# A transformer layer's tail: the last batch's state-space inputs made by channel tiles, its attention moved behind its first scan step, the experts' buffers moved

## The chip, the cores and the metric

The kernel runs on one core of a Trainium2 chip. A core has a matmul engine (TensorE, PE in the profile), a vector engine (VectorE, DVE), an activation engine (ScalarE, ACT), a general engine (GpSimd, POOL), a queue processor for transfers (SyncE, SP), and DMA engines that all of them share. Each engine runs its instructions in the order in which the program lists them, and semaphores hold an instruction until what it needs is done. The metric is the device time of one execution, in microseconds (us).

## The reference, cut to what matters

The input is `x`, 4 batches of 256 tokens with 256 channels. Three parts are added to it in turn, each on a layer norm of the sum so far:

1. A cross-attention of 8 heads: each batch's tokens look at 4096 context rows and at themselves.
2. A routed part. A small router scores the tokens of a batch. The best 64 go through an attention of 16 heads among themselves (`_attn_core`), the other 192 through a state-space layer (`_ssm_core`).
3. A mixture of 8 experts, of which each token takes 2.

```python
def _ssm_core(u, ...):
    xi, z = jnp.split(u @ in_w, 2, axis=-1)              # 512 channels each
    xc = conv_b + sum((xp[:, j:j + L] * conv_w[:, j] for j in range(DC)))
    xc = jax.nn.silu(xc)
    proj = xc @ xproj_w                                  # dtp (16), Bm (16), Cm (16)
    delta = jax.nn.softplus(dtp @ dt_w + dt_b)
    dA = jnp.exp(delta[..., None] * A)
    dBu = (delta * xc)[..., None] * Bm[:, :, None, :]
    # h = dA_t * h + dBu_t over the 192 tokens; y_t = sum over 16 states of h * C_t
    y = jnp.moveaxis(ys, 0, 1) + xc * Dp
    return (y * jax.nn.silu(z)) @ out_w
```

The experts are `silu(x @ gate) * (x @ up)` and then `@ down`, weighted and summed over the two experts of a token. All of it is fp32.

## The kernel before

**Tiling.** Channels or tokens lie on the 128 partitions. The 512 channels of the state-space layer are four channel tiles (`NDT`), m = 0 to 3, of 128 channels by 192 tokens, kept side by side in one tile of 128 x 768 (`xc`, `zs`, `delta`, `y`).

**The planner.** The cross-attention is a hand-written loop over 128 pieces of work. Beside it runs a list of Python generators (`active`), each of which issues some instructions and then yields how much later it is due, and how much room on VectorE its next step asks for. `slot(budget)` gives due generators their turn. The "time" here is only a counter (`now`), which the writer advances by an estimate at each piece. So the yields decide where instructions stand in each engine's order, and nothing else.

**The batches.** `routed(b)` is the generator of one batch's second part: `router`, `ssm_front`, the scan, `ssm_back`. `attention` is a generator beside it. Batches 0 to 2 lie under the cross-attention of the later batches. The last batch's part can only start when the cross-attention ends, and is called `late` in the code. `sortable` and `dispatch` sort the tokens of batches 0 to 2 by expert into 19 blocks of 128 rows (`NB`).

**The tail.** After the cross-attention come two loops. `ordered` runs the 19 sorted blocks. `experts` runs the last batch's 256 tokens through all 8 experts in turn ("dense"); it needs `x4T`, which `prepare` makes at the end of the last batch's second part. The last batch's generators run in the slots of `ordered`. For a block j the steps are:

- `load(j)`: three weight transfers of 512 KB on SP's queue (gateT, upT, downT, L1559), the expert's number read from a register that the block's entry is loaded into; three buffers each.
- `gather(j)`: GpSimd fetches the block's 128 rows (xg, L1597), 4 buffers.
- `turn_block(j)`: two transposes (psxb, L1609) and a copy on ScalarE (xTb, L1612).
- `half(j, 0)` and `half(j, 1)`: gate and up, p0b and p1b (L1618).
- `gated`: a tanh on ScalarE (sg, L1568), two VectorE instructions (L1569, L1573, the result is hb). In this text one such pair on VectorE is a gating.
- `down(j)`: pdb (L1632), a copy yb (L1639), and a store to ysd on SP's queue (L1640). In program order, `down(j - 1)` stands behind the gating of block j, and `load(j + 2)` behind that.

**The last batch before the scan.** `finish_batch` adds the last psx product of the cross-attention (L1392, added at L1400). `router` then normalises the tokens (L183 to L211), transposes them (psxn, L250; xnT, L255), scores them (psh, pssc; gelu at L273), ranks them on VectorE (L278 to L300), counts positions (psn, L306) and permutes (psg, L331), which gives `ua` (L336). `ssm_front` makes psin (L533) for each m, evicts it into xc and zs (L537, L541), adds the convolution (L508), and then works on all four channel tiles at once: tanh (L544) and silu (L546), projection (pspr, L553), the store bcd of B and C (L560), the gate of z (L563, L568), psdt (L579), ReLU and Abs on ScalarE (L586), exp and ln (L591, L592), delta (L594), the y products (L598) and delta times xc (L601). `attention` waits only for `ua`, so it runs in between: psqk (L378), kbd (L395), psva, psas (L419), the softmax (amx, pa, asm), psat, psao, psoT, psad, dsort.

**The late scan.** `ssm_scan_late` does 16 steps, four groups of four states (k) by four channel tiles (m). ScalarE makes the decay (L706), VectorE the rest:

```python
nc.vector.tensor_tensor(db, spread[k, 0], bc(xc[:, m, :], 1, SG), ALU.mult)   # L738
nc.vector.tensor_tensor_scan(out=db, data0=das[i % 2], data1=db, ...)         # L739
nc.vector.tensor_tensor(db, db, spread[k, 1], ALU.mult)                       # L745
nc.vector.tensor_tensor(db[:, :SG//2], db[:, :SG//2], db[:, SG//2:], ALU.add) # L746
```

TensorE sums the states into yps (L714). The rows of B and C come spread over the partitions by DMA from bcd (`spread`, tiles bbl and cbl, L696). `ssm_back` adds yps to y (L761), multiplies by the gate (L764), multiplies by out_w (pssd, L769), permutes back (psback, L779) and adds to x (L784); `prepare` normalises and transposes (psx at L1705).

**Memory.** Pools are laid out one behind the other, and those of the tail (`fp`, `fw`, `fk`, `late`) lie over those of the cross-attention: context rows (`ctx`, 16 KB a partition), then a pool `wk` with keys, values and transposed probabilities.

Of the kernel before, what the change touches and what calls it, by code (L numbers as in the profile page):

```python
# [8 lines left out]
F32 = mybir.dt.float32  # L9
AF = mybir.ActivationFunctionType  # L10
ALU = mybir.AluOpType
# [3 lines left out]
P = 128  # L15
B, T, D = 4, 256, 256
S = 4096
NT = B * T // P
KD = D // P
# [5 lines left out]
NBOT = T - KTOP  # L25
DIN, DS, DC, DTR = 512, 16, 4, 16
NDT = DIN // P
# [19 lines left out]
def perceiver_layer(ctx: ExitStack, tc: tile.TileContext, a: dict, out: bass.AP):  # L47
    nc = tc.nc
# [4 lines left out]
    bg = ctx.enter_context(tc.tile_pool(name="bg", bufs=1))  # L53
# [35 lines left out]
    cs = {}  # L89
# [132 lines left out]
    def bank(name):  # L222
        return ps_m.tile([P, 512], F32, tag="m", name=name)
# [8 lines left out]
    def router(b, st):  # L232
# [1 line left out]
        xb = x_sb[:, 2 * b : 2 * b + 2, :]  # L234
        mv = moments(xb)
        rs = scales(mv, twice=True)
        yield 2.5, 0.4
        nm = offsets(mv, rs)
        one = small.tile([P, 2], F32, name="one")
        nc.vector.tensor_scalar_add(one, rs[:, 0], 1.0)  # L240
        xn2 = bg.tile([P, 2, D], F32, tag="r1", name="xn2")
        scaled(xn2, xb, rs[:, 1], nm[:, 1])
        scaled(xb, xb, one, nm[:, 0])
        yield 2.5, 0

        xnT = bg.tile([P, KD, T], F32, tag="r2", name="xnT")
        ps = bank("psxn")
# [14 lines left out]
            out=lower, in_=lower, compare_op=ALU.is_gt, fill=0.0, base=0,  # L262
            pattern=[[P, 2], [-1, T]], channel_multiplier=1,
        )
        yield 2.0, 0
        hs = bg.tile([P, 2, T], F32, tag="r3", name="hT_srow")
        hT, srow = hs[:, 0, :], hs[:, 1, :]
        ps = bank("psh")
# [2 lines left out]
                ps[:, :T], cs["r_w1"][:, c, :], xnT[:, c, :], start=(c == 0), stop=(c == KD - 1)  # L271
            )
        nc.scalar.activation(hT, ps[:, :T], AF.Gelu_apprx_tanh, bias=cs["r_b1"])  # L273
        yield 3.0, 2.7

        ps = bank("pssc")
        nc.tensor.matmul(ps[:, :T], cs["r_w2"][:, 0, :].to_broadcast([P, P]), hT, start=True, stop=True)
# [10 lines left out]
        for h in range(2):  # L288
            eq = bg.tile([P, T], F32, tag="r4", name="eq")
            for other, op0, op1 in (  # L290
                (lower[:, h, :], ALU.is_equal, ALU.mult), (eq, ALU.is_gt, ALU.add),
            ):
                nc.vector.scalar_tensor_tensor(
                    out=eq, in0=srow, scalar=scol[:, h : h + 1], in1=other, op0=op0, op1=op1
                )
            nc.vector.tensor_reduce(out=rank[:, h : h + 1], in_=eq, axis=AX.X, op=ALU.add)
            if h == 0:
                yield 0.5, 1.6
        top = small.tile([P, 2], F32, name="top")
        nc.vector.tensor_scalar(  # L300
            out=top, in0=rank, scalar1=float(KTOP), scalar2=None, op0=ALU.is_lt
        )
        yield 1.0, 1.4

        ps = bank("psn")
        nc.tensor.matmul(ps[:, 0:1], cs["tri"], top[:, 0:1], start=True, stop=True)  # L306
# [13 lines left out]
        nc.vector.tensor_tensor(  # L320
            perm, bc(cs["posid"], 1, 2), bc(pos, 2, T), ALU.is_equal
        )
        yield 3.0, 0

        while late and "ready" not in order:
            yield 1.0, 0
# [32 lines left out]
    def attention(b, st):  # L359
# [6 lines left out]
        awq = weight("awq")  # L366
        yield early(b), 0
        awk = weight("awk")
        while "ua" not in st:
            yield 2.0, 0  # L370
        ua, dsort = st["ua"], st["dsort"]
        yield 3.0, 0
# [109 lines left out]
    def ssm_front(b, st):  # L482
# [34 lines left out]
        while "ua" not in st:  # L517
            yield 2.0, 0
        ua = st["ua"]
        yield 2.0, 0  # L520
        pss = {}
        for m in range(NDT + 1):
# [38 lines left out]
            out=bcd.rearrange("o s t -> (o s) t"), in_=projT[DTR:, :]  # L561
        )
        nc.scalar.activation(delta, zs, AF.Tanh)  # L563
        if late:
            st["late"] = ssm_scan_late(b, st)
            next(st["late"])
        yield 2.0, 1.0
        nc.vector.scalar_tensor_tensor(  # L568
            out=zs, in0=delta, scalar=1.0, in1=zs, op0=ALU.add, op1=ALU.mult
# [27 lines left out]
        for m in range(NDT):  # L597
            nc.scalar.activation(  # L598
                y[:, m, :], xc[:, m, :], AF.Copy, scale=cs["Dp"][:, m : m + 1]
            )  # L600
        (nc.vector if late else nc.gpsimd).tensor_tensor(xc, xc, delta, ALU.mult)  # L601

    def ssm_scan(b, st):

# [73 lines left out]
    def ssm_scan_late(b, st):  # L678

        SG = 4
        K = DS // SG
        pool = late["pool"]
        xc, delta = st["xc"], st["delta"]
# [14 lines left out]


        def decay(i):
            k, m = divmod(i, NDT)
            if k < K:
                for s in range(SG):
                    nc.scalar.activation(  # L706
                        das[i % 2][:, s, 1:], delta[:, m, 1:], AF.Exp,
                        scale=cs["amat"][:, m, SG * k + s : SG * k + s + 1],
                    )

        def sums(i):
# [12 lines left out]
        zero = pool.tile([P, SG, NBOT], F32, tag="dbl", name="zero", bufs=3)[:, :2]  # L724
        nc.gpsimd.memset(zero, 0.0)
        for i in range(2):
            nc.tensor.matmul(
                yps[:, i, : 2 * NBOT], ident, zero.rearrange("p s t -> p (s t)"),
                start=True, stop=False,
            )  # L730
        yield 0.0, 0
        decay(0)
        yield 1.0, 3.8
        for i in range(K * NDT):
            k, m = divmod(i, NDT)
            decay(i + 1)
            db = dbl[i] = pool.tile([P, SG, NBOT], F32, tag="dbl", name="db", bufs=3)
            nc.vector.tensor_tensor(db, spread[k, 0], bc(xc[:, m, :], 1, SG), ALU.mult)  # L738
            nc.vector.tensor_tensor_scan(  # L739
                out=db.rearrange("p s t -> p (s t)"),  # L740
                data0=das[i % 2].rearrange("p s t -> p (s t)"),
                data1=db.rearrange("p s t -> p (s t)"),
                initial=0.0, op0=ALU.mult, op1=ALU.add,
            )
            nc.vector.tensor_tensor(db, db, spread[k, 1], ALU.mult)  # L745
            nc.vector.tensor_tensor(db[:, : SG // 2], db[:, : SG // 2], db[:, SG // 2 :], ALU.add)  # L746
            if i:
                sums(i - 1)
            if m == NDT - 1:
                load(k + 2)  # L750
            yield 3.9, 3.8
        sums(K * NDT - 1)
        yield 1.5, 0
# [304 lines left out]
    def start(g):  # L1058
        active.append([g, now[0], 0.0])
# [479 lines left out]


    with ExitStack() as s4, tc.manual_schedule():
        fp = s4.enter_context(tc.tile_pool(name="ffn", bufs=1))
        fw = s4.enter_context(tc.tile_pool(name="ffw", bufs=3))
        fk = s4.enter_context(tc.tile_pool(name="ffk", bufs=3))
        ps_g = s4.enter_context(tc.tile_pool(name="ps_g", bufs=3, space=PSUM))
        late["psum"] = s4.enter_context(tc.tile_pool(name="ps_y", bufs=1, space=PSUM))
# [30 lines left out]
        def ordered():  # L1577
# [15 lines left out]

            def gather(j):
                if j < NB:
                    xgs[j] = fp.tile([P, D], F32, tag="xg", name="xg", bufs=4)
                    nc.gpsimd.indirect_dma_start(  # L1597
                        out=xgs[j], out_offset=None, in_=x4d,
                        in_offset=bass.IndirectOffsetOnAxis(
                            ap=order["tokens"][:, j : j + 1], axis=0  # L1600
                        ),
                    )

            def turn_block(j):
# [22 lines left out]
            def down(j):  # L1627
# [12 lines left out]
                nc.sync.dma_start(out=ys[j * P : (j + 1) * P, :], in_=y)  # L1640
                yield 0.86

            for j in range(4):
                gather(j)
            for j in range(3):
                load(j)
            for _ in range(6):
                yield 1.0
            turn_block(0)
            for j in range(NB):  # L1650
                pg = yield from half(j, 0)
                pu = yield from half(j, 1)
                turn_block(j + 1)
                hs[j] = fk.tile([P, NHC, P], F32, name="hb")
                gated(pg, pu, hs[j].rearrange("p m i -> p (m i)"), 512)
                gather(j + 4)
                yield 0.5
                yield from down(j - 1)
                if j:
                    load(j + 2)  # L1660
            yield from down(NB - 1)

            start(collect(NSORT, ys, order["slots"], order["weights"]))
# [168 lines left out]
```

## Time and profile before

| | us |
|---|---|
| median of 3 runs | 1555.44 (1549.75 to 1558.04) |
| the profiled execution | 1555.58, span 1553.9, mean clock 0.977 |
| last values matmul of the cross-attention ends | 1274.15 |
| last batch: last psx product added (L1400) | 1275.53 |
| last batch: ua done | 1308.6 |
| first multiply of the late scan (L738) | 1356.7 |
| last add of the late scan (L746) ends | 1443.1 |
| first matmul of the dense experts (L1749) | 1462.5 |

All stage times are microseconds from the start of the span. In the views of the profile, a row of the stages gives the stretch, its length, and then for each engine its busy time with the number of instructions in brackets. PEclk is the TensorE clock that was granted, as a part of full speed. A row of the chain of waits gives start, length, and the engine, tile and line that the end of the program hung on at that time. PEld is the loading of a matmul's stationary operand. "SPq" is SP's queue of transfers.

### The profile page before, as it was taken

To read this page: it belongs to the slowest core of one execution; us is meant where nothing else is said; L and a number is where in the kernel's file an instruction comes from. 1 tells how busy PE (TensorE), PEld (TensorE's weight loads), DVE (VectorE), ACT (ScalarE), POOL (GpSimd) and SP (SyncE) were. 2 spreads that over 40 slices of the span, in tenths; PEclk is the share of its full clock that TensorE was granted. 3 is DMA by queue.
4 is the path that set the end of the run, shared out by engine and by line. 5 is a ranking of instruction groups with operands and counts; after the bars stand their busy time and mean duration, and the time that the engine had idled before them with its cause. 6 is when DMAs were issued, how large, how long until landed. Compare 5 with 4: busy or idle time off the path is not lost.

```text
span 1553.9 us, 37283 instructions
## 1 busy us (share of the span) xinstructions
PE 1461.9 (94%) x15686; PEld 1039.5 (67%) x15686; DVE 1057.1 (68%) x1812; ACT 758.9 (49%) x1486; POOL 412.0 (27%) x464
## 2 busy tenths in 40 slices
PE   7999999999999999999999999999998868988799
PEld 3757667576667475766665767757665558778587
DVE  1666666666699976565999866658988633499453
ACT  3444454454666644555667454546664413534211
POOL 1000000000089940000799500005996011110100
PEclk9999999999999999999999999999999968999899
DMA  7445543524344525243454343334543115777471
GB/s 240 149 131 160 161 139 107 180 72 143 120 147 140 182 83 192 79 145 100 141 176 158 113 144 126 99 112 162 159 127 114 42 55 183 253 250 259 125 233 48
DMA packets 157767, 223.41 MB, mean 144 GB/s; under 512 B 14976, under 2 KB 76160, under 8 KB 157600
## 3 DMA queue, kind: packets, MB, share of 16 engines
q1 hardware_dynamic: 152368, 211.45, 42.7%
q10 hardware_dynamic: 3744, 5.51, 1.1%
q0 software_dynamic: 1488, 4.07, 0.9%
q8 instruction: 124, 2.03, 0.5%
q14 instruction: 43, 0.35, 0.1%
HBM read 216.56 MB, written 4.42 MB: 142 GB/s over the span
## 4 chain that ended last, share of the span: by engine, by line
PE 63%; POOL 14%; DVE 13%; issue 4%; ACT 3%; DMA 2%; ACTq 0%; SPq 0%; DVEq 0%; POOLq 0%
PE po L1345 12%; PE su L1279 11%; PE psv L1263 11%; PE psk L1226 9%; POOL y L652 5%; POOL db L637 5%; POOL db L650 4%; DVE sp L1299 4%; PE su L1287 2%; PE pg L1749 2%; PE pu L1749 2%; PE pde L1762 2%; DVE pt L1336 2%; DVE db L739 1%; DVE db L644 1%
## 5 line engine op out<-in xcount | busy, mean ns | idle before, releaser
L1299 DVE TENSOR_SCALAR_CACHE_REDUCE sp<-su 128x1088 f32<-128x1088 f32 x256 | 318.8, 1281 | 182.0 <-PE su L1287 182.0
L1336 DVE STREAM_TRANSPOSE pt<-sp 128x1088 f32<-128x1088 f32 x256 | 328.0, 1295 | 57.0 <-PE po L1345 56.9
L1327 ACT ACTIVATE sp<-sp,nb 128x1088 f32<-128x1088 f32 x256 | 305.2, 1195 | 13.9 <-DVE nb L1316 13.7
L1345 PE MATMUL po<-pt,v 128*64 128x128 f32 x4352 | 263.9, 278 | 2.3 <-DVE pt L1336 1.3
L1279 PE MATMUL su<-kt,qz 64*32 64x512 f32 x4096 | 256.0, 609 | 4.4 <-DVE nb L1316 3.7
L1226 PE MATMUL psk<-ctx,wk 128*128 128x512 f32 x512 | 245.1, 612 | 10.2 <-DMA ctx<-in_ctxT 7.7
L1345 PEld LDWEIGHTS po<-pt,v 128*64 128x64 f32 x4352 | 241.7, 139 | 14.1 <-issue 7.7
L1263 PE MATMUL psv<-wv,ctx 128*128 128x128 f32 x2048 | 250.3, 279 | 0.6 <-DMA ctx<-in_ctxT 0.3
L1263 PEld LDWEIGHTS psv<-wv,ctx 128*128 128x128 f32 x2048 | 236.1, 192 | 6.7 <-issue 1.4
L1226 PEld LDWEIGHTS psk<-ctx,wk 128*128 128x128 f32 x512 | 91.4, 191 | 94.3 <-issue 85.0
L1214 ACT COPY kt<-psk 128x512 f32<-128x512 f32 x128 | 74.8, 585 | 158.6 <-PE psk L1226 158.4
L1279 PEld LDWEIGHTS su<-kt,qz 64*32 64x32 f32 x4096 | 63.3, 108 | 124.4 <-issue 93.0
L652 POOL TENSOR_TENSOR y<-y,db 128x192 f32<-128x192 f32 x192 | 135.2, 704 | 15.1
L1267 ACT COPY v<-psv 128x512 f32<-128x512 f32 x144 | 79.2, 558 | 119.8 <-PE psv L1263 118.5
L644 DVE TENSOR_TENSOR_SCAN db<-da,db 128x384 f32<-128x384 f32 x96 | 123.2, 1284 | 14.4 <-POOL db L637 3.7
L650 POOL TENSOR_TENSOR db<-db,cb 128x384 f32<-128x384 f32 x96 | 110.8, 1154 | 26.4 <-DVE da L642 26.4
L395 POOL TENSOR_TENSOR kbd<-qk,hmask 128x512 f32<-128x512 f32 x8 | 8.2, 1045 | 407.1 <-ACT qk L385 407.1
L637 POOL TENSOR_TENSOR db<-bb,xc 128x384 f32<-128x384 f32 x96 | 111.2, 1181 | 0.2
L1287 PEld LDWEIGHTS su<-kt,qz 128*32 128x32 f32 x2048 | 34.6, 109 | 109.3 <-issue 109.3
L632 ACT ACTIVATE da<-delta,A_log_sb 128x192 f32<-128x192 f32 x192 | 75.4, 447 | 51.1 <-DVE da L642 38.4
L1382 ACT COPY ao<-po 128x128 f32<-128x128 f32 x32 | 8.5, 264 | 152.5 <-PE po L1345 152.5
L1311 PEld LDWEIGHTS su<-mq,same 128*128 128x128 f32 x256 | 41.1, 191 | 54.7 <-DVE mq L1306 37.8
(278 smaller groups left out, 1587.2 us busy)
## 6 DMA issues: line engine op xcount, KB each, us to landing
ctx<-in_ctxT SPq DMA_DIRECT2D x256, 512.0 KB, 4.8
gateT<-in_gateT SPq DMA_DIRECT2D x27, 512.0 KB, 4.0
upT<-in_upT SPq DMA_DIRECT2D x27, 512.0 KB, 5.1
downT<-in_downT SPq DMA_DIRECT2D x27, 512.0 KB, 6.2
bb<-bcd SPq DMA_DIRECT2D x24, 192.0 KB, 4.3
cb<-bcd SPq DMA_DIRECT2D x24, 192.0 KB, 3.6
wv<-in_wv SPq DMA_DIRECT2D x32, 128.0 KB, 2.4
in_w<-in_in_w SPq DMA_DIRECT2D x32, 128.0 KB, 3.8
```

Source lines behind the costliest of these rows:

```text
L637: nc.gpsimd.tensor_tensor(db, bbs[k], bc(xc[:, m, :], 1, SG), ALU.mult)
L644: nc.vector.tensor_tensor_scan(out=db, data0=da, data1=db, initial=0.0, op0=ALU.mult, op1=ALU.add,)
L650: nc.gpsimd.tensor_tensor(db, db, cbs[k], ALU.mult)
L652: nc.gpsimd.tensor_tensor(y[:, m, :], y[:, m, :], db[:, s, :], ALU.add)
L1226: nc.tensor.matmul(ps, wqk[G][:, 0, c, :], ct[:, c, :], start=(c == 0), stop=(c == KD - 1),)
L1263: nc.tensor.matmul(ps[:, i * P : (i + 1) * P], lhsT, wv[G][:, w, c, :], start=(c == 0), stop=(c == KD - 1),)
L1267: nc.scalar.copy(v.rearrange("p k d -> p (k d)"), ps[:, : n * P])
L1279: nc.tensor.matmul(su[q * 32 : (q + 1) * 32, SC[j] + lo : SC[j] + lo + 512], qT[r, j, s * 32 : (s + 1) * 32], kt[r, q, lo : lo + 512], sta ...
L1299: nc.vector.tensor_scalar(out=sps[n][j], in0=su[:, SU[j] : SU[j] + QK], scalar1=1.0, scalar2=None, op0=ALU.mult, op1=ALU.max, accum_out=nm ...
L1327: nc.scalar.activation(sps[n][j], sps[n][j], AF.Exp, bias=nbs[n][:, j : j + 1], accum_out=lss[b][:, hp, s, j : j + 1],)
L1336: nc.vector.transpose(pts[m, j][:, i, :], sps[n][j])
L1345: nc.tensor.matmul(pos[m][j * HD : (j + 1) * HD, :], vts[m // 2, k // 4][:, k % 4, j * HD : (j + 1) * HD], pts[m, j][:, :, kk * 32 : (kk + ...
```

## The change

It has five parts, all in the tail.

1. `router`'s last call is due sooner at each yield (0.9 for 2.5 and the like), one yield in the ranking is left out, and one is longer (4.5 for 1.0).
2. `ssm_front` hands the last batch to a new function, `front_late`. It does convolution, tanh and silu for each channel tile. ReLU moves from ScalarE to VectorE (with the bias, L670 of the changed file). The projection, bcd, psdt, Abs, exp and ln follow, and the loads of `spread` behind ln. Then for each channel tile comes an add (delta) and a product into a tile of its own, `u`. The gate of z and the y products leave the front; `gate_late` makes them in the sixth step of the scan.
3. `attention` of the last batch waits until the scan has been started (`scanning`), not only for `ua`.
4. The scan multiplies by `u`, where it took `xc`.
5. The pool of the experts' weights (`fw`) is laid out ahead of `fp`, so over the context rows and what follows them. The gathered rows xg lie in the tiles bb and cb that `dispatch` used (`scratch`). In `ordered` the first loads are named ahead of the first gathers, six yields ahead of the first block are left out, and `gather(j + 4)` and half of `down(j - 1)`'s matmuls move ahead of `gated`.

```diff
 def router(b, st):
-        yield 2.5, 0.4
+        yield (0.9 if late else 2.5), 0.4
...
-            if h == 0:
+            if h == 0 and not late:
                 yield 0.5, 1.6
...
-        yield 1.0, 1.4
+        yield (4.5 if late else 1.0), 1.4
...
 def attention(b, st):
-        while "ua" not in st:
+        while ("scanning" if late else "ua") not in st:
             yield 2.0, 0
...
 def ssm_front(b, st):
         ua = st["ua"]
+        if late:
+            yield from front_late(b, st, ws, conv)
+            return
...
+    def front_late(b, st, ws, conv):
+        ua, xc, zs, delta = st["ua"], st["xc"], st["zs"], st["delta"]
+        pool = late["pool"]
+        th = pool.tile([P, NDT, NBOT], F32, tag="ul", name="th")
...
+        st["dt_w"] = pool.tile([DTR, DIN], F32, name="dt_wl")
+        nc.scalar.dma_start(out=st["dt_w"], in_=a["dt_w"])
+        yield 0.9, 0
+        for m in range(NDT + 2):
+            if m < NDT:
+                ps = pss[m] = bank("psin")
...
+                nc.scalar.activation(
+                    xc[:, m, :], ps[:, :NBOT], AF.Identity, bias=cs["conv_b"][:, m : m + 1],
+                    scale=cs["conv_w"][:, m, DC - 1 :],
+                )
+                nc.scalar.activation(zs[:, m, :], ps[:, NBOT : 2 * NBOT], AF.Copy, scale=0.5)
+            if 1 <= m <= NDT:
+                conv(m - 1, pss[m - 1])
+                nc.scalar.activation(th[:, m - 1, :], xc[:, m - 1, :], AF.Tanh)
+            if m >= 2:
+                silu(m - 2)
+            yield 0.9, 0
...
+        nc.scalar.copy(projT, ps[: DTR + 2 * DS, :NBOT])
...
+        nc.scalar.dma_start(
+            out=bcd.rearrange("o s t -> (o s) t"), in_=projT[DTR:, :]
+        )
+        st["late"] = ssm_scan_late(b, st)
+        yield 0.9, 0
+        ev = bg.tile([P, NDT, NBOT], F32, tag="y", name="ev")
+        for i in range(2):
+            ps = bank("psdt")
...
+            for j in range(2):
+                m = 2 * i + j
+                v = ps[:, j * NBOT : (j + 1) * NBOT]
+                nc.scalar.activation(ev[:, m, :], v, AF.Abs, bias=cs["dt_b"][:, m : m + 1])
+                nc.vector.tensor_scalar(
+                    out=delta[:, m, :], in0=v, scalar1=cs["dt_b"][:, m : m + 1], scalar2=0.0,
+                    op0=ALU.add, op1=ALU.max,
+                )
+        nc.scalar.activation(ev, ev, AF.Exp, scale=-1.0)
+        nc.scalar.activation(ev, ev, AF.Ln, bias=1.0)
+        next(st["late"])
+        yield 5.4, 0
+        u = st["u"] = pool.tile([P, NDT, NBOT], F32, tag="ul", name="ul")
+        for m in range(NDT):
+            nc.vector.tensor_tensor(delta[:, m, :], delta[:, m, :], ev[:, m, :], ALU.add)
+            nc.vector.tensor_tensor(u[:, m, :], xc[:, m, :], delta[:, m, :], ALU.mult)
+            if m == 0:
+                next(st["late"])
+        st["scanning"] = True
+
+    def gate_late(b, st):
+        xc, zs = st["xc"], st["zs"]
+        tz = bg.tile([P, NDT, NBOT], F32, tag="y", name="tz")
+        nc.scalar.activation(tz, zs, AF.Tanh)
+        yield 2.0, 1.0
+        nc.vector.scalar_tensor_tensor(
+            out=zs, in0=tz, scalar=1.0, in1=zs, op0=ALU.add, op1=ALU.mult
+        )
...
+        for m in range(NDT):
+            nc.scalar.activation(
+                y[:, m, :], xc[:, m, :], AF.Copy, scale=cs["Dp"][:, m : m + 1]
+            )
...
 def ssm_scan_late(b, st):
         decay(0)
-        yield 1.0, 3.8
+        yield 0.0, 3.8
+        u = st["u"]
...
-            nc.vector.tensor_tensor(db, spread[k, 0], bc(xc[:, m, :], 1, SG), ALU.mult)
+            nc.vector.tensor_tensor(db, spread[k, 0], bc(u[:, m, :], 1, SG), ALU.mult)
...
+            if i == 5:
+                start(gate_late(b, st))
...
+        fw = s4.enter_context(tc.tile_pool(name="ffw", bufs=3))
         fp = s4.enter_context(tc.tile_pool(name="ffn", bufs=1))
-        fw = s4.enter_context(tc.tile_pool(name="ffw", bufs=3))
...
-                    xgs[j] = fp.tile([P, D], F32, tag="xg", name="xg", bufs=4)
+                    xgs[j] = scratch(j, [P, D], "xg")
...
+            for j in range(3):
+                load(j)
             for j in range(4):
                 gather(j)
-            for j in range(3):
-                load(j)
-            for _ in range(6):
-                yield 1.0
             turn_block(0)
             for j in range(NB):
                 pg = yield from half(j, 0)
                 pu = yield from half(j, 1)
                 turn_block(j + 1)
+                gather(j + 4)
+                rest = down(j - 1)
+                yield next(rest, 0.9)
+
                 hs[j] = fk.tile([P, NHC, P], F32, name="hb")
                 gated(pg, pu, hs[j].rearrange("p m i -> p (m i)"), 512)
-                gather(j + 4)
-                yield 0.5
-                yield from down(j - 1)
+                yield from rest
```

More of the change, by code (lines that the diff above doesn't have):

```diff
@@ L243, in router @@
         scaled(xb, xb, one, nm[:, 0])
-        yield 2.5, 0
+        yield (0.9 if late else 2.5), 0
         xnT = bg.tile([P, KD, T], F32, tag="r2", name="xnT")
@@ L264, in router @@
         )
-        yield 2.0, 0
+        yield (0.9 if late else 2.0), 0
         hs = bg.tile([P, 2, T], F32, tag="r3", name="hT_srow")
@@ L273, in router @@
         nc.scalar.activation(hT, ps[:, :T], AF.Gelu_apprx_tanh, bias=cs["r_b1"])
-        yield 3.0, 2.7
+        yield (1.8 if late else 3.0), 2.7
         ps = bank("pssc")
@@ L322, in router @@
         )
-        yield 3.0, 0
+        yield (1.8 if late else 3.0), 0
         while late and "ready" not in order:
@@ L563, in ssm_front @@
         nc.scalar.activation(delta, zs, AF.Tanh)
-        if late:
-            st["late"] = ssm_scan_late(b, st)
-            next(st["late"])
         yield 2.0, 1.0
@@ L600, in ssm_front, with silu @@
             )
-        (nc.vector if late else nc.gpsimd).tensor_tensor(xc, xc, delta, ALU.mult)
+        nc.gpsimd.tensor_tensor(xc, xc, delta, ALU.mult)
+    def front_late(b, st, ws, conv):
+        ua, xc, zs, delta = st["ua"], st["xc"], st["zs"], st["delta"]
+        pool = late["pool"]
+        th = pool.tile([P, NDT, NBOT], F32, tag="ul", name="th")
+        pss = {}
+        def silu(m):
+            nc.vector.scalar_tensor_tensor(
+                out=xc[:, m, :], in0=th[:, m, :], scalar=1.0, in1=xc[:, m, :],
+                op0=ALU.add, op1=ALU.mult,
+            )
[6 more added lines that the diff above has]
+                for j in range(2):
+                    for c in range(KD):
+                        nc.tensor.matmul(
+                            ps[:, j * NBOT : (j + 1) * NBOT], ws[m][:, j, c, :],
+                            ua[:, c, :NBOT], start=(c == 0), stop=(c == KD - 1),
+                        )
[10 more added lines that the diff above has]
+            yield 0.9, 0
+        projT = bg.tile([DTR + 2 * DS, NBOT], F32, tag="projT", name="projT")
+        ps = bank("pspr")
+        for m in range(NDT):
+            nc.tensor.matmul(
+                ps[: DTR + 2 * DS, :NBOT], cs["xproj"][:, m, :], xc[:, m, :],
+                start=(m == 0), stop=(m == NDT - 1),
+            )
+        nc.scalar.copy(projT, ps[: DTR + 2 * DS, :NBOT])
+        bcd = st["bcd"] = dram.tile([2, DS, NBOT], F32, tag="bcd", name="bcd")
+        nc.scalar.dma_start(
[6 more added lines that the diff above has]
+            ps = bank("psdt")
+            for j in range(2):
+                m = 2 * i + j
+                nc.tensor.matmul(
+                    ps[:, j * NBOT : (j + 1) * NBOT], st["dt_w"][:, m * P : (m + 1) * P],
+                    projT[:DTR, :], start=True, stop=True,
+                )
+            for j in range(2):
+                m = 2 * i + j
+                v = ps[:, j * NBOT : (j + 1) * NBOT]
[3 more added lines that the diff above has]
+                    op0=ALU.add, op1=ALU.max,
+                )
+        nc.scalar.activation(ev, ev, AF.Exp, scale=-1.0)
[9 more added lines that the diff above has]
+        st["scanning"] = True
@@ new lines, in gate_late @@
+    def gate_late(b, st):
[3 more added lines that the diff above has]
+        yield 2.0, 1.0
+        nc.vector.scalar_tensor_tensor(
+            out=zs, in0=tz, scalar=1.0, in1=zs, op0=ALU.add, op1=ALU.mult
+        )
+        yield 2.0, 0
+        y = st["y"] = bg.tile([P, NDT, NBOT], F32, tag="y", name="y")
+        for m in range(NDT):
+            nc.scalar.activation(
+                y[:, m, :], xc[:, m, :], AF.Copy, scale=cs["Dp"][:, m : m + 1]
+            )
@@ L684, in ssm_scan_late @@
         pool = late["pool"]
-        xc, delta = st["xc"], st["delta"]
+        delta = st["delta"]
         spread = {}
@@ L1653, in ordered @@
                 turn_block(j + 1)
+                gather(j + 4)
+                rest = down(j - 1)
+                yield next(rest, 0.9)
                 hs[j] = fk.tile([P, NHC, P], F32, name="hb")
                 gated(pg, pu, hs[j].rearrange("p m i -> p (m i)"), 512)
-                gather(j + 4)
-                yield 0.5
-                yield from down(j - 1)
+                yield from rest
                 if j:
                     load(j + 2)
+            yield 0.9
             yield from down(NB - 1)
```

## The prediction

> **What bounds the kernel now.** I read the page's busy row and slices first, then the busy times by stage, then the chain of waits through the last 280 us, because the change touches only what comes after the cross-attention.
>
> ```profile
> PE 1461.9 (94%) x15686; PEld 1039.5 (67%) x15686; DVE 1057.1 (68%) x1812; ACT 758.9 (49%) x1486; POOL 412.0 (27%) x464
> PE   7999999999999999999999999999998868988799
> DVE  1666666666699976565999866658988633499453
> PEclk9999999999999999999999999999999968999899
> ```
>
> 94% of TensorE says nothing about the tail: the last ten digits of the PE row fall to 6, and the DVE digits rise to 9 just there. The stages (PE, PEld, DVE, ACT, POOL busy, then clock, DMA share, GB/s):
>
> ```profile
> 1240.00:1274.20 34.20, 27.22 (x230) 20.98 (x214) 15.18 (x37) 4.73 (x9) 0.00 (x0) 0.62 0.00 0
> 1274.20:1308.60 34.40, 24.18 (x142) 21.96 (x142) 10.31 (x28) 11.69 (x22) 8.06 (x10) 0.85 0.64 215
> 1308.60:1356.70 48.10, 45.61 (x308) 39.60 (x308) 17.66 (x31) 24.40 (x57) 7.24 (x10) 0.96 0.67 222
> 1356.70:1443.10 86.40, 76.12 (x532) 69.20 (x531) 81.49 (x89) 35.73 (x97) 9.26 (x7) 1.00 0.79 256
> 1443.10:1462.50 19.40, 10.71 (x45) 7.35 (x45) 6.13 (x14) 4.79 (x10) 4.80 (x6) 0.87 0.48 147
> 1462.50:1553.90 91.40, 86.81 (x392) 75.43 (x392) 41.26 (x104) 13.63 (x34) 6.56 (x7) 0.97 0.39 126
> ```
>
> They are the end of attention; the last batch's router up to ua (1308.6); its state-space front up to the scan's first multiply (1356.7); the scan; its way out into the dense experts' input; the dense experts. The nineteen sorted blocks fill TensorE beside the middle three. TensorE is not full in any of these four, VectorE is 94% busy in the scan, and the dense stage can't start before the last batch has come through. So the tail's length is **this one chain**: 34.4 + 48.1 + 86.4 + 19.4, then 91.4. One step of the scan in the chain of waits, and the next one's start:
>
> ```profile
> 1391.10 0.88 DVE db L738
> 1392.01 1.77 DVE db L739
> 1393.80 0.97 DVE db L745
> 1394.79 0.56 DVE db L746
> 1395.35 0.88 DVE db L738
> ```
>
> A step is 4.25 us of VectorE. Where a block's gating (L1569, L1573: 0.68 + 0.69 us) lies between, it is 5.7. The start of the sorted blocks, and a line of the wait list:
>
> ```profile
> 1274.41 5.31 DMA xg<-x4d,tokens
> ...
> 1280.96 3.78 PE p0b L1618 x16
> ```
>
> ```profile
> SPq L1559 <- PE po L1345: 16.8, 1, 16.8
> ```
>
> The gathered rows land at 1279.7, and the first block runs at half speed; SP's queue stood 16.8 us before the first gateT load, until the last values matmul (1274.15).
>
> **What the Trainium skill says.** "TensorE: Matmul & The Clock Gate" (Part 1, the HAM clock gate): after an idle window of some 3.4 us the array runs at half clock until busy for about as long. The trace agrees: after 4.4 us idle the sixteen p0b took 3.78 us, later ones 1.95. "ScalarE: Activation LUTs" (What ACT_TABLE_LOAD costs): 1283 ns a load and a drain of 1380 on top. Here the load is 1.28 us, and from the end of a tanh (1290.51) over the load to the gelu (1291.82) it is 1.31, so I charge 1.28. "DMA: Bandwidth & Descriptors" (Issuing engines are not separate DMA queues): all queues share sixteen engines. The trace doesn't contradict it (slices of up to 404 GB/s in the scan); I use it below.
>
> **The change, part by part.** I took the order from the instruction lists of both programs, and durations from the trace of before.
>
> *Buffers.* xg moves to dispatch's tiles. In the changed program its gathers wait only for dispatch's results (done at 1258.7), so the 5.31 us leaves the path. The first gateT load, though, still waits for the last values matmul. It leaves at 1274.15 as now, and lands 3.8 us later (the shortest gateT landing) at 1278.0. So block 0 starts 3.0 us earlier, not 6. TensorE's order changes too: the last psx matmul (now 1274.8, its add at 1275.5) stands behind block 0's p0b and half its p1b. With 3.2 us idle before, the clock may be warm or cold: 1.8 to 3.8 us, then 0.9 to 1.8. I take the middle, 2.7 + 1.3, plus 0.7 for psx. Its add is at 1282.7, **7.2 us later** (5.7 to 8.7); the router, waiting for it, is late by as much.
>
> *Router.* From that add to ua is 33.1 us now. New: normalised rows 3.6; second scaling and xTb copy 1.4; xnT 1.05; tanh table, tanh, gelu table, gelu 3.65; pssc 0.7; ranks 4.5 (5.9 now, as a gating lies in it); then gating's first half 0.7, half a p1b 0.9, psn 0.8, positions 1.8; the rest of p1b, a transpose and pdb end 1.1 after that; psg and ua 2.8. Sum 23.0: ua at 1305.7, 3 us earlier than now. TensorE waits 2 us for the normalised rows; no DMA is in it.
>
> *Front.* From ua to the scan's first multiply is 48.1 us now, with the attention's exp and its table, one ln table, four y products and whole-tile steps in it. New, per channel tile: the four psin with half-block matmuls between, 8.1; eviction 0.9; the last conv behind gating 3 on VectorE 4.2; tanh, silu 0.9; pspr, copy 1.8; half a p1b and psdt 1.4; four Abs 1.4; exp and ln with two tables 4.2; four spread-load issues on ScalarE's queue 1.8; an xTb copy, the tanh table, tanh 2.2 (gating 4 stands ahead of delta on VectorE); gating 1.4. Then four adds and four products of 192. None of that shape is in the trace; "VectorE: DVE Perf Modes" (The TRN2 errata) gives (N+151)/0.96 ns for an fp32 add, hence an estimate of 0.36 us each (nearest row, conv's 0.41), 2.9 together. Sum 31.2: **first multiply at 1337.0**, 19.7 us earlier. The spread loads, issued at 1328.6 to 1330.4, land in 4 to 5 us, before it. dt_w's load on ScalarE's queue has 15 us. ReLU moved to VectorE hides under the tables. The xTb copy behind all this makes TensorE wait some 3 us at block 5: hidden, as VectorE is the bound next. Error: 3 us either way.
>
> *Scan.* Now: sixteen steps 68.0, eleven gatings 15.6, oa and dsort 0.5: 84.1 for 86.4, factor 1.027. New between first multiply and last add: 68.0; thirteen gatings 18.5; and the attention with the gate of z, which came before the scan: amx, pa, asm, its reciprocal, zs, oa, dsort, 3.9. Sum 90.4, times 1.027 is 92.9. TensorE between its first and last yps sum gets 85 us of matmuls (blocks at 5.7, sums 0.7, attention 6), so both engines are nearly full. Walking the fifteen gaps between sums in both lists (TensorE 5.1 to 7.0 us each, the longest where psqk or psao lie; VectorE 5.7, but 4.25 without a gating and 7.6 where asm and zs lie), psas comes 0.9 late for amx, and oa makes psoT wait 0.6; else each hb finds its p1b, if only 0.3 us ahead at gating 8. I add 1.1: **94.0**, 7.6 more. ScalarE gets 5.6 us more (qk, pa, tz, y, paT and others), 42 of 94: room. POOL's kbd pair (2.0 us) moves behind three gathers that have three blocks of lead. awv and awo move behind a decay on ScalarE's queue, with over 10 us to land. Weights, gathers and spread loads make 27.4 MB in 94 us, 291 GB/s against 256: higher, not full.
>
> *Way out and dense stage.* Same instructions in the same order after the last add, the 8.0 us landing of ysd and the gather of yg included: 19.4 + 91.4, cost nothing either way.
>
> Sum: −19.7 + 7.6 = −12.1. The profiled execution took 1555.58 us (span 1553.9 and 1.7 around it), the median is 1555.44. 1555.58 − 12.1 gives **1543.5**.
>
> **Rivals.**
> *The same within 0.5%.* The front's gain is eaten by weight loads. A block's load is issued behind the ysd store of two blocks before: copy 0.4, store and register loads 1.6, landing 4.0 make about 6 us, against 6.2 us of TensorE work in that time. No p0b waits for a DMA now. At 291 GB/s the landing could grow by a microsecond; half a microsecond in each of thirteen blocks is 6.5 us: 1550.0.
> *Slower.* VectorE and TensorE close into a ring in the scan. A gap in which the gating waits for a p1b standing behind the same gap's sum lasts 0.7 + 0.9 + 1.8 + 1.4 + 4.25 = 9.0 us, against 5.7. Should TensorE trail 2.5 us more (the wait at block 5, cold clock), seven such gaps give 23 us: 1567. It decides from a scan of 106 us, 6.6 a step. Against it: three db buffers, and a gating one block behind.
> *The change does what its words say.* The weights come at 1257.3, block 0 starts at 1274.9 warm, and psx at 1278: 4 us better, 1539. Against it stands the wait in the program.
>
> **How the numbers follow.** Forecast 0.62, ring 0.11, weight loads 0.21, early weights 0.06. Start 1.5, front 3 and scan 4 us either way, and the runs' own 1549.75 to 1558.04, put the forecast between 1535 and 1551; with half of the weight-load case above it, 1534 to 1553. 0.5% (7.8 us) is about what a measurement of this kernel can tell from no change. Faster 0.68, same 0.21, slower 0.11.
>
> **What would show it.** In the profile after: the first xg gathers before 1265 and gateT still at 1274.15; psx's last add near 1282.7; ua near 1305.7; the first scan multiply (L838 in the changed file) near 1337; 94 us to the last halving add (L846), with VectorE over 95% busy and TensorE over 90%; 19.4 us to the dense stage, and 91.4 after it. The sum is wrong if the first multiply comes after 1342, if a scan step takes 6.6 us, or if p0b waits for a DMA in the scan.

## The result, and the profile after

The changed kernel took **1548.56 us** (median of 20 runs, 1542.66 to 1558.2), the kernel before 1554.78 (20 runs, 1548.87 to 1558.04). The ratio is 0.9965, 95% interval 0.9951 to 0.9979: 0.35% faster, 6 us. The prediction said 1543.5, so the gain is half of the forecast 12.1 us, and within the 0.5% that it called no change. (The time lies inside the stated range of 1534 to 1553 us, but that range took in half of the weight-load rival as well.) The profiled execution took 1548.97 us (span 1547.3).

Part of the busy rows and slices on the page of the changed kernel:

```profile
PE 1458.9 (94%) x15686; PEld 1039.8 (67%) x15686; DVE 1059.8 (68%) x1825; ACT 757.8 (49%) x1485; POOL 410.6 (27%) x464
...
PE   7999999999999999999999999999998968889799
...
DVE  1666666666599976565899866757999554589553
...
PEclk9999999999999999999999999999999979999999
```

They look like those of before: a row of tenths doesn't show six microseconds. The stages do. These are the same six, with the borders where the same events lie in the changed kernel (last values matmul, ua, first multiply, last add, first dense matmul):

```profile
1240.00:1273.60 33.60, 24.02 (x230) 18.72 (x230) 18.04 (x45) 4.96 (x8) 3.96 (x4) 0.72 0.06 16
1273.60:1306.60 33.00, 25.03 (x159) 22.88 (x158) 11.76 (x30) 12.79 (x25) 5.45 (x9) 0.90 0.66 216
1306.60:1335.85 29.25, 26.62 (x167) 23.70 (x166) 12.82 (x33) 16.45 (x37) 1.90 (x2) 0.94 0.58 189
1335.85:1438.68 102.83, 92.34 (x661) 84.48 (x660) 87.32 (x99) 41.69 (x113) 11.60 (x11) 0.98 0.79 260
1438.68:1456.38 17.70, 10.73 (x45) 7.19 (x44) 6.25 (x14) 4.77 (x10) 4.81 (x6) 0.92 0.56 180
1456.38:1547.30 90.92, 86.33 (x392) 75.22 (x392) 41.30 (x104) 13.61 (x34) 6.53 (x7) 0.97 0.39 127
```

| stage | before | predicted | after |
|---|---|---|---|
| last values matmul to ua | 34.4 | 31.5 | 33.0 |
| ua to first multiply | 48.1 | 31.2 | 29.25 |
| first multiply at | 1356.7 | 1337.0 | 1335.85 |
| scan | 86.4 | 94.0 | **102.8** |
| way out | 19.4 | 19.4 | 17.7 |
| dense experts | 91.4 | 91.4 | 90.9 |

Everything ahead of the scan came close to the walk: the add 0.9 us later, the front 2 us shorter, the first multiply 1.15 us earlier. The scan is 8.8 us longer than forecast. VectorE is busy 87.3 of its 102.8 us (85%, forecast over 95%), and its wait list for the scan says for what. The columns are total, number, longest:

```profile
DVE sg L1672 <- ACT sg L1671: 12.2, 7, 5.2
...
PE p0b L1721 <- DMA gateT<-in_gateT: 6.9, 3, 3.9
```

The gating waits 12.2 us for a tanh. The tanh waits for p0b, and p0b three times for its weights, which the prediction named as what would make its sum wrong. The longest of these waits in the timeline (start, length, engine, line; "q" marks the issue of a transfer):

```profile
1325.72 1.89 PE L1735 MATMUL pdb<-downT,hb 128*128 128x256 f32 x8
...
1331.66 0.37 ACT L1742 COPY yb<-pdb 128x256 f32<-128x256 f32 x1
...
1332.05 0.34 SPq L1743 DMA_DIRECT2D ysd<-yb  x1
...
1333.18 0.38 SPq L1662 DMA_DIRECT2D gateT<-in_gateT  x1
...
1333.59 0.47 ACTq L479 DMA_DIRECT2D out_w<-in_out_w  x1
...
1341.27 3.54 PE L1721 MATMUL p0b<-xTb,gateT 128*128 128x128 f32 x16 [3.94 <-DMA gateT<-in_gateT]
```

pdb is done at 1327.6. Its copy yb stands behind ln, an xTb copy, a table load and a tanh on ScalarE and comes 4.05 us later; the store waits for yb, and the next gateT load stands behind the store on SP's queue. It leaves at 1333.18, out_w's two loads leave right behind it on ScalarE's queue, and it lands 7.95 us later. TensorE idled 3.94 us, and then took 3.54 us for a p0b of 1.95, because the clock had gone down: the granted clock is 0.55 over these 3.5 us.

Two theories came out of this. **Burst**: the loads of the scan's first steps share the DMA engines with 1.3 MB that nobody needs yet (out_w, and the spread rows of the second four states). **Place in the queue**: the weight load is issued too late, behind the store of ysd. The rival to both was the ring of TensorE and VectorE, in which no DMA has a part.

### The profile page after: what moved, and what is told of

The parts are those of the page before. It is cut to its first block, busy times and chain, and to the rows that moved or that the text cites. A ratio compares the mean times of both kernels' runs of the same rounds, so it can differ in the third digit from the quotient of the medians.

```text
span 1547.3 us, 37278 instructions
## 1 busy us (share of the span) xinstructions
PE 1458.9 (94%) x15686; PEld 1039.8 (67%) x15686; DVE 1059.8 (68%) x1825; ACT 757.8 (49%) x1485; POOL 410.6 (27%) x464
## 4 chain that ended last, share of the span: by engine, by line
PE 64%; POOL 15%; DVE 10%; DMA 4%; issue 4%; ACT 2%; SPq 0%; ACTq 0%; DVEq 0%; POOLq 0%
PE po L1447 12%; PE su L1381 11%; PE psv L1365 11%; PE psk L1328 9%; POOL y L751 5%; POOL db L736 5%; POOL db L749 5%; DVE sp L1401 3%; PE su L1389 2%; PE pg L1853 2%; PE pu L1853 2%; PE pde L1866 2%; PE p1b L1721 2%; DMA gateT<-in_gateT 2%; DVE db L743 1%
## 5 line engine op out<-in xcount | busy, mean ns | idle before, releaser
L1401 DVE TENSOR_SCALAR_CACHE_REDUCE sp<-su 128x1088 f32<-128x1088 f32 x256 | 318.8, 1281 | 182.0 <-PE su L1389 181.8
L1447 PEld LDWEIGHTS po<-pt,v 128*64 128x64 f32 x4352 | 240.9, 139 | 13.9 <-issue 7.5
```

Of the source, the lines that this page charges most:

```text
L1401: nc.vector.tensor_scalar(out=sps[n][j], in0=su[:, SU[j] : SU[j] + QK], scalar1=1.0, scalar2=None, op0=ALU.mult, op1=ALU.max, accum_out=nm ...
L1447: nc.tensor.matmul(pos[m][j * HD : (j + 1) * HD, :], vts[m // 2, k // 4][:, k % 4, j * HD : (j + 1) * HD], pts[m, j][:, :, kk * 32 : (kk + ...
```

## The experiments

The last values matmul of the cross-attention ends at another time in each profiled execution (1270.6 to 1278.3), so the table counts from there: "psx add" and "first multiply" are microseconds after that end, "scan" and "way out" (last add of the scan to the first dense matmul) are lengths, and T is the time from that end to the first dense matmul. Each kernel was timed beside the kernel before (medians 1552.8 to 1554.8 us), and its ratio is to that. "Cold" and "warm" stand for matmuls at about half and at full clock.

| kernel | ratio (95%) | psx add | first multiply | scan | way out | T |
|---|---|---|---|---|---|---|
| before | 1 | 1.4 | 82.6 | 86.4 | 19.4 | 188.4 |
| changed | 0.9965 (0.9951 to 0.9979) | 10.0 | 62.2 | 102.8 | 17.7 | 182.8 |
| e1: second spread pair and out_w later | 0.9937 (0.9924 to 0.9950) | 9.9 | 62.2 | 97.7 | 17.8 | 177.7 |
| e10: out_w alone later | 0.9942 (0.9920 to 0.9964) | 10.1 | 62.4 | 97.7 | 17.5 | 177.6 |
| e2: ysd on ScalarE's queue | 0.9918 (0.9903 to 0.9933) | 9.0 | 62.0 | 95.1 | 15.7 | 172.9 |
| e9: gateT, upT ahead of the store | 0.9899 (0.9876 to 0.9921) | 10.4 | 62.7 | 95.1 | 15.7 | 173.5 |
| e3: e1 and e2 | 0.9910 (0.9894 to 0.9926) | 10.1 | 62.3 | 95.2 | 15.7 | 173.2 |
| e4: psx ahead of block 0 | 0.9945 (0.9932 to 0.9958) | 1.4 | 58.9 | 98.0 | 20.0 | 177.0 |
| e5: first weights early | 0.9941 (0.9926 to 0.9956) | 4.7 | 57.4 | 103.1 | 18.1 | 178.6 |
| u1: parts 1 to 4 | 0.9946 (0.9933 to 0.9959) | 1.4 | 54.2 | 96.9 | 30.9 | 182.0 |
| u2: part 5 | 1.0131 (1.0114 to 1.0149) | 10.1 | 99.9 | 88.8 | 18.0 | 206.8 |
| e7: e2, e5 and psx earlier | 0.9871 (0.9855 to 0.9888) | 3.8 | 55.4 | 96.3 | 15.0 | 166.6 |
| e8: e7 and e1 | **0.9848** (0.9823 to 0.9874) | 3.8 | 55.4 | 93.5 | 14.9 | 163.8 |
| e11: e8 with e9 for e2 | 0.9849 (0.9823 to 0.9874) | 3.8 | 54.6 | 94.4 | 14.9 | 163.9 |

### The burst: e1 and e10

```diff
         load(0)
-        load(1)          # e1 only: at i == 1 of the scan
...
-        st["ow"] = [stream(out_w ...) for i in range(2)]   # both: at i == 9 of the scan
```

> The changed kernel, but the second pair of spread loads (bbl and cbl of k = 1) leaves in the scan's second step and not with the first pair, and out_w's two loads leave in the scan's tenth step and not ahead of its first; nothing else is moved. Theory 'burst' (the weight loads of the first scan steps share the sixteen DMA engines with 1.3 MB of loads that aren't needed yet, so gateT takes 7.95 and 6.79 us to land): the first of these lands in about 5 us, the 3.9 us wait of p0b and its cold matmuls (3.5 for 1.8 us) go, the second wait shrinks too; the scan falls from 102.8 us to 96 to 98, the kernel to about 1543. Theory 'place in the queue' (gateT is issued too late, behind the ysd store, whatever else moves): gateT still comes 2 us or more after TensorE is free, the scan stays above 101 us and the kernel at 1547 to 1549.

Measured: scan 97.7, 1544.31 us, as "burst" said. Which of the two loads it was:

> The changed kernel, with nothing but out_w's two loads (0.5 MB) moved from before the scan's first step to its tenth step; the spread loads all leave together as in the changed kernel. In the earlier run both were moved, and the scan fell by 5.2 us. If the burst is a matter of bytes, out_w is 0.5 of 1.3 MB, and its issue is the one at the very moment (0.4 us behind gateT): the first wait of 3.9 us falls to 1.5 to 2.5, the scan to 99 to 101, the kernel to 1545 to 1547. If out_w does nothing, 1548.5; if it is all of it, 1544.

Measured: scan 97.7 and 1544.37 us with out_w alone, all of e1's gain and more than the share by bytes that I had expected. No gain is seen from the spread pair: p0b waits 0.7 us for weights in e1 and 3.4 in e10, but the gating waits 6.5 us in both. In e10's timeline the same gateT load and its p0b:

```profile
1333.36 0.38 SPq L1668 DMA_DIRECT2D gateT<-in_gateT  x1
...
1338.73 2.02 PE L1727 MATMUL p0b<-xTb,gateT 128*128 128x128 f32 x16 [1.23 <-DMA gateT<-in_gateT]
```

The issue is as late as before (0.2 us later), but p0b starts 5.4 us behind it and not 8.1, and after 1.23 us of idling the clock is still up (granted 1.00): 2.02 us, not 3.54. So 2.7 us of landing and 1.5 us of clock hang on 0.5 MB in another engine's queue. "DMA: Bandwidth & Descriptors" (Issuing engines are not separate DMA queues) says that transfers run on the same sixteen DMA engines and interleave, whichever engine started them; the 2.7 us are what that cost here.

### The place in the queue: e2, e3 and e9

```diff
-                nc.sync.dma_start(out=ys[...], in_=y)
+                nc.scalar.dma_start(out=ys[...], in_=y)     # e2, e3
...
                 gated(pg, pu, ...)
+                load(j + 2)      # e9: gateT and upT here
                 yield from rest
-                load(j + 2)      # e9: only downT here, behind the store
```

> The changed kernel, but the ysd store is issued on ScalarE's queue behind the copy yb; SP's queue holds only the weight loads. Theory 'place in the queue': gateT of block j+2 leaves when block j-1's matmuls have freed its buffers, 4 to 6 us earlier than now; no p0b of the scan waits over 0.5 us for a DMA; scan 95 to 97 us, kernel about 1542. Theory 'burst': the same bytes share the engines, the landing grows from 5 to 8 or more us, but has more lead; the first wait (behind the spread loads and out_w) stays at 2 us or more, scan 98 to 101, kernel 1545 to 1547. The store's issue takes about 0.35 us of ScalarE's queue 19 times; if that delays tanh or the decay the gain is lost.

> Both edits of the two runs before: the early spread loads and out_w later, and the ysd store on ScalarE's queue. If DMA is the whole of the scan's excess over my 94 us, the scan comes to 93 to 96 us with VectorE over 95% busy, and the kernel to about 1540. If the scan stays over 99 us with no p0b or p1b waiting for a DMA, the cause lies in the ring of TensorE and VectorE (psqk, psva, psao in the same gaps), and not in DMA.

> The changed kernel, ysd still on SP's queue, but gateT and upT of block j+2 are issued ahead of the second half of down(j-1) and its ysd store; only downT stays behind the store. This tells 'place in the queue' from the other thing that the run with the store on ScalarE's queue changed (no stores among SP's loads at all). If the place is what counts: gateT and upT leave about one step of the block loop earlier (3 to 5 us), p0b waits under 1.5 us in all for weights, scan 95 to 98 us, kernel 1541 to 1543. If it is the stores that slow SP's queue: gain under 2 us, 1547.

e2 took 1540.89 us, e3 1538.04, e9 1538.46; their scans are 95.1, 95.2 and 95.1 us, and no p0b of the scan waits for a DMA. VectorE is 92% busy in them, not over 95%. The timeline of e2 for the same block; the first line is the load that this p0b reads, by the program's instruction list:

```profile
1318.07 0.38 SPq L1662 DMA_DIRECT2D gateT<-in_gateT  x1
...
1331.99 0.37 ACT L1742 COPY yb<-pdb 128x256 f32<-128x256 f32 x1
...
1338.21 2.05 PE L1721 MATMUL p0b<-xTb,gateT 128*128 128x128 f32 x16 [1.32 <-ACT xTb L1715]
```

This gateT leaves 13.9 us ahead of the yb behind whose store it stood in the changed kernel, 15 us earlier than there (I had expected 4 to 6), and p0b waits for its copied rows only. The next gateT load, which does leave beside the spread loads (1328.93), takes 10.4 us to land, and its p0b at 1347.52 has no wait for it. In e9 the same load and its p0b are:

```profile
1324.02 0.38 SPq L1663 DMA_DIRECT2D gateT<-in_gateT  x1
...
1342.27 1.95 PE L1728 MATMUL p0b<-xTb,gateT 128*128 128x128 f32 x16
```

e9 keeps the store on SP's queue, and the load leaves 14 us earlier than in the changed kernel (counted from the values' end), so it is the place of the load that counts, not a queue without stores. The median landing of gateT is *longer* in e2 and e9 (6.0 and 5.9 us) than in the changed kernel (4.9 in the same stretch): the loads have lead enough not to care. e3 adds nothing to e2's scan, and its gating waits the same 4.0 us: with that lead, moving out_w buys nothing. Both theories hold, as two cures of one lateness, and the place is the larger one (7.7 of the 8.8 us against 5.1). "DVE sg" waits in e2's scan:

```profile
DVE sg L1672 <- ACT sg L1671: 4.0, 5, 2.6
```

This 4.0 is the most that the ring and ScalarE's order cost without weight waits; the ring rival is no more than that. e2's way out is 2.0 us shorter as well: the chain of the changed kernel runs through the landing of the last ysd store (6.7 us), that of e2 through the last batch's own pssd and normalisation.

### The start: e4 and e5

```diff
+            for _ in range(3):       # e4
+                yield 1.0
             turn_block(0)
...
+        fw0 = s4.enter_context(tc.tile_pool(name="ffw0", bufs=1))   # e5: every third load
-        fw = s4.enter_context(tc.tile_pool(name="ffw", bufs=3))
+        fw = s4.enter_context(tc.tile_pool(name="ffw", bufs=2))
```

> The changed kernel, with three yields ahead of block 0, so that the last psx matmul stands ahead of block 0's p0b in TensorE's order, and runs while TensorE waits for the first weights. Its add comes at about 1275.5 (1283.6 in the changed kernel) and the scan's first multiply 6 to 8 us earlier, near 1329. Theory 'DMA in the scan': the weight loads are pressed as before, one block more lies in the scan, and the scan takes 103 to 106 us: kernel 1543 to 1546. If all of the earlier start reached the end: 1541. If the scan takes it all back (TensorE is the bound from 1278 to the end of the sorted blocks, so an earlier chain doesn't help): 1548.

> The changed kernel, but the three tiles of the first block's weights have a pool of their own that covers only the context rows (every third load goes into it; the other two sets stay in ffw, with two buffers each). So block 0's weights need not wait for the last values matmul; all later loads keep their order. This is what the change's words say, my rival 'early weights'. If it holds: gateT leaves near 1257, p0b starts within 1.5 us of the last values matmul and is warm (2 us, not 3.75), psx's add comes 5 us earlier (4.9 us after the values end, 9.9 in the changed kernel), and the first multiply 4 to 5 us earlier. The scan keeps its waits for weights (103 us, give or take 3). Kernel 1544 if the start reaches the end, 1548.5 if the scan takes it back.

e4 took 1545.32 us. That is inside its forecast, but by two misses that cancel: less of the early start was left, and the scan was shorter (98.0 us, where I had expected 103 to 106). The add comes 8.5 us earlier, but the first multiply only 3.3. The chain of waits shows where 5 us went:

```profile
1290.93 2.05 PE p0b L1721 x16
1292.98 2.68 issue
1295.66 2.85 PE p1b L1721 x16
```

With the new order the ranking stands ahead of gating 0 on VectorE, and gating 0 comes late. p0b and p1b share three buffers, and p1b of block 1 starts 0.09 us after the gating's first instruction ends; the profile itself names no releaser ("issue"). TensorE idles 2.68 us and runs cold after it (this p1b and the next pdb take 2.8 us more than warm). The scan is 4.8 us shorter: its p0b wait 2.1 us for weights in place of 6.9. By the timeline out_w leaves 2.5 us behind the gateT load there, not 0.4, and p0b starts after 1.43 us of idling, warm; that fits e10, but was not tried by itself. In e5 block 0's weights do come early (gateT leaves at 1244.7): its add is at 4.7 us, 5.3 earlier, and the first multiply 4.8 earlier. The scan has the same waits for weights (6.8 us of p0b) and takes 103.1; the kernel takes 1544.27 us, as expected. So an earlier start reaches the end (T 4.2 us less), and the start and the scan's loss are separate matters.

### The parts: u1 and u2

u1 is the kernel before with parts 1 to 4, u2 the kernel before with part 5.

> Only parts 1 to 4 of the change (router's yields, the front by channel tiles, attention behind the scan's start, u); pools, gathers and the loop over the sorted blocks as before. psx stands ahead of block 0 again (its add 1.4 us after the values end), and block 0 waits for the gathers until 6.8 us after the values end. By my steps: router 23 to 25 us from the add, front 31, first multiply 57 us after the values end (62 in the changed kernel); one block more in the scan, loads pressed as now: scan 103 to 106; kernel 1546 to 1549. If the part 5 that is left out was worth anything, this is above the changed kernel's 1548.6 by that; if it cost (psx behind block 0), below.

> Only part 5 (pools, xg, order in the loop over the sorted blocks); router, front, attention and scan as before. By my steps: psx's add 8 us later than before (behind one and a half cold blocks), router 33 and front 48 us as before: first multiply 5 to 8 us later than before's 82.6 us after the values end; scan about 85 us with one to two blocks fewer in it. Kernel 1558 to 1562. If TensorE were the bound of the tail, the blocks that start 3 us earlier would bring it to 1552.

u1 took 1543.52 us, less than the whole change; u2 took 1572.72. **Part 5 by itself costs 20 us**, and nothing is seen of a gain from it on top of the others (0.9946 without it, 0.9965 with it; the intervals overlap a little). u2's first multiply is 17 us later than before's, where I had expected 5 to 8: 6.3 of it by ua, with psx's add 8.6 late, and 10.9 between ua and the multiply. There TensorE is busy 51.8 us in place of 45.6 (337 matmul records, against 308); how the rest divides was not tried. In u1 the scan takes 96.9 us, less than the 103 to 106 I had expected, and ends early, but its way out is long:

```profile
1423.86:1454.76 30.90, 27.94 (x180) 24.79 (x181) 11.19 (x27) 8.75 (x17) 0.00 (x0) 1.00 0.55 181
```

TensorE is busy 27.9 of these 30.9 us, with sorted blocks that are still to do (180 matmul records, against 45 in the changed kernel's 17.7 us). Parts 1 to 4 bring the last batch forward so far that TensorE's own work becomes the end. So u1 and the changed kernel reach nearly the same T by opposite ways (182.0 and 182.8). u1's dense stage is 4.3 us shorter: it starts warm (the first three groups of four matmuls take 1.03 us each, against 2.07, 1.92 and 1.30 in the changed kernel), and 0.95 us of its work (pslg) has been done before.

### Together: e7, e8 and e11

> Three edits together: block 0's weights in their own pool, the ysd store on ScalarE's queue, and one yield ahead of block 0, so that psx stands behind half a block and not behind one and a half. With the store's edit alone the kernel took 1540.9 us, and TensorE was busy 51.4 of the 62 us from the last values matmul to the first multiply, some 3 of them at half clock. If TensorE is the bound from the end of attention to the last sorted block, nearly all of what it idles or runs cold at the start comes off: 6 to 7 us, 1534 to 1535. If the last batch's chain is the bound, its add comes 6 us earlier and the gain is about the same, but the scan stays at 95 us. If VectorE's ranking in front of a gating makes p1b wait (as it did with three yields) half of it goes: 1538.

> The best kernel so far (1531.4: block 0's weights in their own pool, ysd on ScalarE's queue, psx behind half a block) with the later spread loads and out_w besides. In that run ScalarE's queue stood at out_w's issue until a downT load had landed (9.6 us in the chain of waits), and the decay, the xTb copy behind it and p0b with it: 3.5 us of waiting on ScalarE, 3.8 us of idle TensorE and a cold p0b. If the wait goes and nothing takes its place: 4 to 5 us less, 1527. If TensorE is full otherwise (it was busy 140 of 152 us): 1528 to 1530. If the scan's first multiply waits for other things: 1531.

> As the run before it, but with gateT and upT ahead of the store on SP's queue in place of the store on ScalarE's queue (19 issues of 0.35 us less for ScalarE in the tail). If ScalarE's issues cost nothing: the same as the run before it, within 1.5 us; if they delay tanh and decay: 2 us better. If downT, still behind the store, is late for pdb: 2 to 4 us worse.

e7 took 1531.41 us: below its forecast, as its gains add up (T is 16.1 us less than the changed kernel's; e2's share is 9.9 and e5's 4.2, and the last 2 us, with psx half a block earlier, were not tried alone). Its chain of waits held something new:

```profile
1318.74 9.56 DMA downT<-in_downT
1328.33 0.39 ACTq L479
...
1330.56 3.09 PE p0b L1725 x16
```

ScalarE could not issue the second half of out_w before a downT load of SP's queue had landed: in the program's instruction list its issue waits for the semaphore that this downT signals. The decay, the xTb copy and p0b stood behind it, for 3.5 us on ScalarE and a cold p0b. e8 moves out_w and the second spread pair: scan 93.5, T 2.8 us less, 1530.54 us. The forecast of 4 to 5 us was too high; in the medians the step is 0.9 us, which the intervals can't tell from nothing. e11 took 1530.40 us: it makes no difference then which of the two cures of the place is taken. e8 and e11 beat both kernels of this case: 1.5% under before.

## Why the prediction was wrong

- **Buffers.** Right: the first gather at 1261.4, and gateT held until the last values matmul. psx's add came at 1283.58, 0.9 later than said, as block 0's p0b ran cold (3.75 us, after 3.20 us idle) where I took the middle of warm and cold. e5 shows that the wait belonged to the pool's extent, since a pool over the context rows alone has none; the add's delay is 8.5 us against before (7.2 said), and e4 and e5 give 3.3 and 4.8 of it back.
- **Router.** 23.0 us said and measured (1283.58 to 1306.60).
- **Front.** 31.2 said, 29.25 measured. The 192-wide adds and products took the estimated 0.35 to 0.36 us. First multiply 1.15 us before the forecast.
- **Scan: the step that failed.** 94.0 said, 102.8 measured. VectorE's work was nearly right: 102.8 less 12.2 of waiting is 90.6, said 92.9. The term "I add 1.1" for waits was 12.2. For it I let each hb find its p1b, from a walk through TensorE's and VectorE's lists in which no weight load had a place; the only ground for leaving them out was that no p0b waits for a DMA in the kernel before. Without weight waits (e2, e3, e9) the scan takes 95.1 to 95.2. That the walk's 94.0 is so near this is partly luck: in e2 the gating waits 4.0 us, not 1.1, and the rest is 91.1, not 92.9.
- **Why that term was wrong.** The budget for a load, 0.4 + 1.6 + 4.0 against 6.2 us, was in the text, as the rival "the same within 0.5%". Two of its terms were mis-sized at one place. The copy was not 0.4 us after pdb, but 4.05 + 0.37, behind the front's ln, an xTb copy and a tanh with its table on ScalarE; the landing was not 4.0 but 7.95, with out_w behind it. I had said of the bandwidth "higher, not full": true as a mean (260 GB/s), and no answer for the few microseconds in which the front's loads and the weights meet. The rival's size came out by chance (1550.0 against 1548.56), not by its form: not half a microsecond in thirteen blocks, but three waits, the first of 3.94 us with a cold p0b behind it.
- **Ring.** It costs 4.0 us of VectorE's time at most (e2), and the 95.1 us scan there is far from the 106 us at which it would decide.
- **Way out.** Said at no cost; it was 1.7 us shorter, and the dense stage 0.5. The sum closes: −1.15 + 8.83 − 1.7 − 0.5 = +5.5, from 1541.8 to 1547.3.

What stays open: how much of out_w's effect is bytes and how much the order in which the engines serve the queues; and whether part 5 is worth something once the loads are early, since u1 was not run with e2 or e9.

## What to carry to other kernels

A prefetch is as early as the last thing in front of it on its queue: count its lead from the slowest engine that this thing waits for, at the worst place, not from the average step. When a stretch of work is moved forward, list the transfers that it brings with it and look for those that nobody needs soon; 0.5 MB at the wrong moment cost 4 to 5 us here. And when a change has parts, build each alone: one of these cost 20 us alone, and no gain from it was seen on top of the others.

## What the hardware showed that was not expected

- How long TensorE may idle before a p0b runs cold was not one length here. After 1.23 to 1.65 us p0b was warm (2.02 to 2.05 us), after 3.1 us and more slowed (3.65 after 3.14 in e2, 3.75 after 3.20, 3.54 after 3.94). Between them the same p0b, behind ScalarE's late xTb copy, took 3.00 us after 2.29 us of idling in the changed kernel (granted clock 0.65), but 2.05 after the same 2.29 us in e5, and 2.05 after 2.54 us in e2. The 3.4 us that the prediction cites from "TensorE: Matmul & The Clock Gate" (Part 1, the HAM clock gate) is no lower bound here.
- A transfer's issue on ScalarE can wait for a transfer of another queue to land, where the program ties both to one semaphore, and holds up all of ScalarE's work behind it (3.5 us in e7).
